# Two transformer blocks on one core: the last eight heads of block one divided by products with ones, and a denser start

## The chip, the cores and the metric

One NeuronCore of a Trainium2 chip runs the whole program; the other cores are idle. The metric is the device time of one execution in microseconds (us), and lower is better. All arithmetic is in float32. The engines are named as the profile names them: PE (TensorE; PEld is its weight load), DVE (VectorE), ACT (ScalarE), POOL (GpSimd), and SP, whose queue issues most of the transfers.

## The reference, cut to what matters

The input x is 2 x 1024 x 256, and a context of 2 x 64 x 256 goes with it. Two blocks follow each other, both with 16 heads of 16 channels:

```
# block 0
q = ln(x);                x = x + self_attention(q, q)             # 16 heads, softmax over 1024 keys
x = x + cross_attention(ln(x), ln(ctx))                            # 64 keys
h = ln(x); logits = h @ rw.T; top 2 of 8 experts, softmax gates
x = x + sum_k gate_k * (gelu(h @ fc1[e_k].T + b1) @ fc2[e_k].T + b2)
# block 1
x = x + self_attention(ln0(x));  x = x + cross_attention(ln1(x), ctx, mask)
x = x + gelu(ln2(x) @ fc1.T + b1) @ fc2.T + b2
```

A head's attention is exp(scores - largest) @ V, divided by the row's sum of exp. The division is what one part of the change computes in another way.

## The kernel before, in words

**Self-attention** (`self_attention`, used by both blocks as layer 0 and layer 1). Four heads are worked on at once: each has 32 rows of the 128, 16 of them channels. A "head group" h is four heads by 512 queries; there are 16 groups per block (batch, half of the queries, four groups of heads), and each has eight cells of 128 keys (or 128 queries by half the keys in the first pass), so 128 cells per block. A cell has three parts:

- pass "a" (L747): four products of queries and keys, whose only use is the largest score of each row; DVE reads each from a PSUM bank with a reduction (L754). It runs `LEAD` = 10 cells ahead of pass "b".
- pass "b" (L758): four products whose exp ACT writes to SBUF (L764). The largest score has been subtracted from the queries' tile (`largest`, L702 turns the maxima, L704 subtracts).
- `product` (L809): exp times V, where V has a column of ones at place 16 of its 20 columns, so that row 16 of each 32 is the sum of exp. ACT copies the sum (L818 the first, L821 the others), and POOL, or DVE once there are no more maxima to take, adds it to the group's accumulator `acc` (L822).

**The division before.** When a group is done, `finish` sends `acc` to DRAM (`send`, L470 and L471). After two groups it is gathered back with the heads side by side (L475); the sums are inverted on DVE (L486), go to DRAM (L487), come back spread over their heads' rows (`spread_out`, L491), and one multiplication divides (L497, on POOL while maxima are taken, else on DVE). `project` then multiplies by the output weights (L426) and adds to x (L434). The steps are put one cell apart by `at_cell`.

**What fills the gaps.** PE, DVE, ACT and SP are issued in the order in which the Python code records them (POOL's order is left to a scheduler). All other work is generators in a `Stream`: values, keys and queries of later groups (L594, L624), the norms (L358), the cross-attention (`weigh`: L1051, L1081, L1117, L1130, L1140, L1155), the dispatch of tokens to experts (`dispatch_task`) and the experts' slots (L1592 first layer, L1622 second). A generator yields its cost in us after a piece, or a wait (zero or less). In the loop over cells, `step` takes pieces by their due time as long as the budget `owed` lasts. Behind the loop `rest` empties the stream by rank and by the waits. `early` with `fill_up` does the same for the first ten cells of pass "a", which have no pass "b" beside them.

**Ends of the attention.** After cell 127 of block 0, only slot 0 of the experts can run at once: slots 1 to 4 need the counts of dispatch 2 (`found` 3), the rest need dispatch 3, which needs the last cross-attention, which needs the projection of the last two head groups (14 and 15).

The cross-attention already divides by products: `product(g)` at L1130 to L1149 multiplies by a 0/1 matrix `picks` to get the sums and inverts them, and `divided` (L1155, L1162) spreads the inverse by another 0/1 product.

Of the kernel before, what the change touches and what calls it, by code (L numbers as in the profile page):

```python
# [41 lines left out]
F32 = mybir.dt.float32  # L42
# [62 lines left out]


O_SUM, O_HEAD = 0, 128
NPICK = 640

W_O, W_V, W_Q, W_K = 0, 512, 1024, 1536  # L110
NSELF = 2048
# [17 lines left out]
class Stream:  # L129
# [46 lines left out]
    def rest(self, later, cell, mark=None):  # L176

        now, ready = 0.0, {}  # L180
        while (self.tasks or later) and (mark is None or mark not in self.made):
            for c in sorted(later):
                if (c - cell) * CELL <= now:
                    for go in later.pop(c):
                        go()
            tasks = [t for t in self.tasks if self.made.issuperset(t.after)]
            able = [t for t in tasks if ready.get(t, 0.0) <= now]
            if able:
                t = max(able, key=lambda t: (t.rank, -ready.get(t, 0.0)))
                cost = self.advance(t)  # L190
                if cost is not None:
                    now += max(0.0, cost)
                    ready[t] = now - min(0.0, cost)
            else:
                now = min([ready[t] for t in tasks] + [(c - cell) * CELL for c in later])
        return now
# [3 lines left out]
def two_blocks(  # L200
# [295 lines left out]
    def divide(dst, by):  # L496
        helper().tensor_tensor(dst, dst, by, ALU.mult)  # L497
# [17 lines left out]
    def self_attention(layer, tail, heads, arrive, extra, when_ready, beside=None):  # L515
# [30 lines left out]
        def at_cell(cell, go):  # L546
            later.setdefault(cell, []).append(go)
# [160 lines left out]
        def finish(h, cell):  # L708


            b, qh, g = h // 8, h // 4 % 2, h % 4
            if g == 0:
                ot[b, qh] = opool.tile([P, 2, 512], F32, tag="ot", name=f"ot_{names}{b}{qh}")
            if g % 2 == 0:
                sm = small.tile([P, 32], F32, tag="sums", name=f"sums_{names}{h}")
                sums[g // 2] = next_heads(), sm
            n, sm = sums[g // 2]
            dst = ot[b, qh][:, g // 2, :]
            send(acc.pop(h), n, g % 2, sm)
            if g % 2 == 1:  # L720
                by = opool.tile([P, 512], F32, tag="by", name=f"by_{names}{h}", bufs=1)
                gather(n, dst)
                at_cell(cell + 1, lambda: invert(n, sm))
                at_cell(cell + 2, lambda: spread_out(n, by))
                at_cell(cell + 3, lambda: divide(dst, by))
                if g == 3:
                    at_cell(cell + 4, lambda: project(b, qh))

        def project(b, qh):
            def go():  # L730
                for t0 in range(0, 4, 2):
                    yield from project_task(ot[b, qh], w, b * TB + 4 * qh + t0, t0, 2)
                when_ready(b, qh, stream, now[0])

            stream.add(go(), 4.0, last=now[0] + 4, rank=60)

        def score(kind, cell, j):
            h, n = divmod(cell, 8)
# [140 lines left out]
        add_values(1, 34, [("norm", 1)] + (["filled"] if layer == 0 else []))  # L879
        if layer == 0:  # L880

            fill_up(-LEAD, 2.0)
            owed = 0.0
            for ahead in range(0, LEAD, 2):
                cell = now[0] = ahead - LEAD
                for n, _ in enumerate(early(ahead)):
                    for go in later.pop(cell + n, []):
                        go()
                    if (ahead, n) == (6, 1):
                        collect(0)  # L890
                        stream.add(largest(0), 0.75, last=cell, mark=("QB", 0))
                        fill_up(cell, 1.0)
                        stream.until(("QB", 0))

                    owed += 0.7
                    while owed > 0.6 and (cost := stream.step(cell)):
                        owed -= cost
        owed = 0.0
# [143 lines left out]
    def weigh(layer, b, pool, w, name, held):  # L1042
# [124 lines left out]
        SC, LA, TU, PR, DI = scores, largest, weights_turned, product, divided  # L1167
        if maxima[0]:

            for now in (  # L1170
                ((SC, 0, 0), (LA, 0, 0)),
                ((LA, 0, 1),),
                ((SC, 0, 1), (LA, 0, 2)),
                ((TU, 0, 0), (LA, 0, 3)),
                ((SC, 1, 0), (LA, 1, 0)),
                ((TU, 0, 1), (LA, 1, 1)),
                ((PR, 0),),
                ((SC, 1, 1), (LA, 1, 2)),
                ((TU, 1, 0), (LA, 1, 3)),
                ((DI, 0),),  # L1180
                ((TU, 1, 1),),
                ((PR, 1),),
            ):
                for step, *args in now:
                    step(*args)
                us = {SC: cost, TU: 1.15, PR: 1.1, DI: 0.55}.get(now[0][0])
                if us:
                    yield us
                yield 0.0
            return  # L1190
        for step, *args, wait in (
            (SC, 0, 0, None),
# [751 lines left out]
def _layout(inputs):  # L1944
# [84 lines left out]
    for r in range(4):  # L2029
        for u in range(2):  # L2030
            for c in range(4):
                picks[SK * u : SK * (u + 1), O_SUM + 32 * r + 8 * c + 2 * r + u] = 1.0
    for c in range(4):
        for h in range(8):
            at = O_HEAD + c * P + DH * h
            picks[32 * c + h, at : at + DH] = 1.0
# [42 lines left out]
```

## Time and profile before

| what | value |
|---|---|
| time, median of 4 runs | 1637.29 us (1633.3 to 1640.46) |
| the profiled execution's own time | 1643.58 us |
| its span, first to last instruction | 1641.8 us |
| mean granted TensorE clock | 0.977 |
| PE busy | 1588.6 us (97%) |
| DVE busy / ACT busy / POOL busy | 981.8 / 911.3 / 414.7 us |
| first product of pass "b" in block 0 (L758) | 61.99 us |
| last product of block 0's attention (L809) begins | 596.58 us, for 3.24 us |
| first product of the last cross-attention of block 0 (L1051) | 638.18 us |

"Busy" of PE counts a matmul from its start to a modelled end, so it does not tell how fast PE went; the granted clock beside it does. A float32 matmul of the program stands in the trace as two records, so four matmuls are "x8". In the timelines each line has the start, the length, the engine, the line of the kernel, the operation with its tiles, the count, and in brackets the idle time before it and what ended that.

### The profile page before, as it was taken

Reading aid. Unit: us, or ns where it says so; the run is one execution under the profiler, and the core shown is the slowest. Engines: PE = TensorE matmul, PEld = TensorE weight load, DVE = VectorE, ACT = ScalarE, POOL = GpSimd, SP = SyncE. Lnnn points to the kernel's source line nnn. Section 1 sums busy time; section 2 is a strip of 40 time slices with the busy share of each in tenths; the row PEclk is TensorE's granted clock in tenths of the full one; section 3 lists DMA queues with packets and bytes.
Section 4 is the critical chain, followed back from the end, with each engine's and each line's share of the span. In section 5 each row is a group of like instructions: output and inputs, shape, how many; then the busy total and the mean of one; then the engine's idle time right before and its main releaser. Section 6 shows DMA issues by size and latency. Waiting matters only on the chain.

```text
span 1641.8 us, 28274 instructions
## 1 busy us (share of the span) xinstructions
PE 1588.6 (97%) x10682; PEld 875.4 (53%) x10682; DVE 981.8 (60%) x2092; ACT 911.3 (56%) x1768; POOL 414.7 (25%) x549
## 2 busy tenths in 40 slices
PE   7999999999999988999999989999999999999998
PEld 3333344444443446778888753344444435546766
DVE  5687857688687737431114456876767777845400
ACT  2277867667665763423322327876776676674321
POOL 2134324234334302141112032411322323321010
PEclk8799999999998999999999999999999999999999
DMA  4333510110000115176556321000110002000000
GB/s 142 123 131 114 180 35 21 27 34 31 30 21 27 60 56 194 68 259 224 180 200 237 97 65 34 21 28 14 40 40 21 21 14 82 15 14 21 14 13 26
DMA packets 56591, 122.09 MB, mean 74 GB/s; under 512 B 12546, under 2 KB 26756, under 8 KB 56068
## 3 DMA queue, kind: packets, MB, share of 16 engines
q1 hardware_dynamic: 52612, 110.08, 20.6%
q0 software_dynamic: 3456, 9.51, 1.6%
q8 instruction: 86, 1.41, 0.4%
q10 hardware_dynamic: 384, 0.66, 0.2%
q14 instruction: 53, 0.43, 0.1%
HBM read 72.14 MB, written 39.42 MB: 68 GB/s over the span
## 4 chain that ended last, share of the span: by engine, by line
PE 91%; DVE 6%; issue 1%; DMA 1%; ACT 1%; another core or an unknown queue 0%; POOL 0%; SPq 0%; DVEq 0%; POOLq 0%; ACTq 0%
PE banks L758 17%; PE banks L747 15%; PE banks L809 14%; PE banks L1592 8%; PE banks L1622 8%; PE banks L624 4%; PE banks L1764 3%; PE banks L1752 3%; PE banks L426 3%; PE banks L594 2%; PE banks L1051 2%; DVE mx_s L754 2%; PE banks L1081 2%; PE banks L1117 2%; PE banks L358 1%
## 5 line engine op out<-in xcount | busy, mean ns | idle before, releaser
L754 DVE TENSOR_REDUCE mx_s<-banks 128x1 f32<-128x512 f32 x1024 | 634.5, 682 | 211.1 <-PE banks L747 206.2
L764 ACT ACTIVATE pt_s<-banks 128x512 f32<-128x512 f32 x1024 | 531.0, 608 | 151.2 <-PE banks L747 125.9
L747 PE MATMUL banks<-KS,QS 16*128 16x512 f32 x2048 | 535.7, 632 | 3.8 <-issue 1.9
L758 PE MATMUL banks<-qb_s,KS 32*128 32x512 f32 x2048 | 509.9, 620 | 8.9 <-DVE qb_s L704 4.9
L822 POOL TENSOR_TENSOR acc_s<-acc_s,part_s 128x512 f32<-128x512 f32 x143 | 181.7, 1270 | 432.8 <-ACT part_s L821 420.9
L758 PEld LDWEIGHTS banks<-qb_s,KS 32*128 32x128 f32 x2048 | 177.1, 185 | 182.5 <-DVE mx_s L754 104.7
L809 PE MATMUL banks<-pt_s,v_s 128*20 128x512 f32 x2048 | 262.2, 604 | 0.7 <-DVE sc_c L1102 0.5
L747 PEld LDWEIGHTS banks<-KS,QS 16*128 16x128 f32 x2048 | 197.5, 186 | 78.5 <-issue 36.4
L1622 PE MATMUL banks<-w_slot,h_s 128*128 128x256 f32 x640 | 145.0, 383 | 2.9 <-ACT h_s L1598 2.9
L809 PEld LDWEIGHTS banks<-pt_s,v_s 128*20 128x20 f32 x2048 | 42.6, 98 | 181.8 <-ACT pt_s L764 129.6
L1622 PEld LDWEIGHTS banks<-w_slot,h_s 128*128 128x128 f32 x640 | 121.8, 192 | 23.5 <-ACT h_s L1598 3.3
L821 ACT COPY part_s<-banks 128x512 f32<-128x512 f32 x157 | 93.8, 598 | 61.7 <-PE banks L809 49.9
L1631 DVE SCALAR_TENSOR_TENSOR ys<-banks,gate,b 128x256 f32<-128x256 f32 x40 | 19.3, 484 | 169.9 <-PE banks L1622 166.9
L1598 ACT ACTIVATE h_s<-banks,w_slot 128x256 f32<-128x256 f32 x104 | 43.6, 470 | 119.0 <-issue 65.3
L1637 POOL DMA_INDIRECT results<-ys,to x40 | 38.7, 967 | 258.4 <-DVE ys L1631 176.3
L1592 PE MATMUL banks<-xsT,w_slot 128*128 128x256 f32 x416 | 95.7, 381 | 0.7 <-ACT xsT L365 0.7
L1592 PEld LDWEIGHTS banks<-xsT,w_slot 128*128 128x128 f32 x416 | 77.3, 190 | 14.8 <-DVE mx_s L754 2.3
L624 PE MATMUL banks<-xT_s,w_att 128*128 128x512 f32 x128 | 69.1, 676 | 0.0
L1755 ACT ACTIVATE h_f<-banks,w_ff 128x512 f32<-128x512 f32 x32 | 22.0, 687 | 73.9 <-PE banks L1752 73.9
L1102 POOL TENSOR_TENSOR sc_c<-sc_c,mx_c 128x512 f32<-128x512 f32 x38 | 39.5, 1042 | 77.6 <-DVE mx_c L1101 77.6
L1764 PE MATMUL banks<-w_ff,h_f 128*128 128x256 f32 x256 | 58.7, 387 | 0.0
L1598 ACT ACTIVATE h_s<-banks,spare 128x256 f32<-128x256 f32 x56 | 23.4, 471 | 63.2 <-issue 31.3
(260 smaller groups left out, 1646.8 us busy)
## 6 DMA issues: line engine op xcount, KB each, us to landing
w_slot<-in_ff_w_dram SPq DMA_DIRECT2D x40, 576.0 KB
sorted_rows<-fill SPq DMA_DIRECT2D x36, 520.0 KB
w_slot<-in_ff_w_dram SPq DMA_DIRECT2D x26, 514.0 KB
whole<-acc_s SPq DMA_DIRECT2D x32, 256.0 KB
spare<-in_ff_w_dram SPq DMA_DIRECT2D x14, 514.0 KB
xs<-sorted_rows SPq DMA_DIRECT2D x20, 260.0 KB
ot_s<-whole SPq DMA_DIRECT2D x16, 256.0 KB
by_s<-turns SPq DMA_DIRECT2D x16, 256.0 KB
```

Source lines behind the costliest of these rows:

```text
L624: nc.tensor.matmul(p, lhsT=w[:, at + k * D + pair * P : at + k * D + (pair + 1) * P], rhs=xT[b][:, k, blk * 512 : (blk + 1) * 512], start= ...
L747: nc.tensor.matmul(sc, lhsT=QS[h % 4][r, qc * P : (qc + 1) * P], rhs=K[r, kh * 512 : (kh + 1) * 512], start=True, stop=True,)
L754: return i, lambda: nc.vector.tensor_reduce(mx[h][:, qc, j, kh : kh + 1], sc, AX.X, ALU.max)
L758: nc.tensor.matmul(sc, lhsT=K[r, n * P : (n + 1) * P], rhs=QB[h][r, :], start=True, stop=True)
L764: nc.scalar.activation(pt, sc, AF.Exp, scale=SCALE)
L809: nc.tensor.matmul(o[32 * j : 32 * j + VW, :], lhsT=V[b][:, cell % 8, 4 * g + j, :], rhs=exps.pop((cell, j)), start=(cell == cells[0]), st ...
L821: nc.scalar.copy(part, o)
L822: helper().tensor_tensor(acc[h], acc[h], part, ALU.add)
L1592: nc.tensor.matmul(ph[:, n, :], lhsT=w[:, at : at + P], rhs=xT[:, k, :], start=(k == 0), stop=(k == 1),)
L1598: nc.scalar.activation(h1[:, f, :], ph[:, n, :], AF.Gelu, bias=w[:, W_B1 + f : W_B1 + f + 1])
L1622: nc.tensor.matmul(py, lhsT=h1[:, f, h * P : (h + 1) * P], rhs=w[:, f * D : (f + 1) * D], start=(f == 0), stop=(f == 7),)
L1764: nc.tensor.matmul(py[:, n, :], lhsT=h1[:, f, t * P : (t + 1) * P], rhs=w2[:, f * D : (f + 1) * D], start=(f == 0), stop=(f == 7),)
```

## The change

Five things, with all else the same:

1. Head groups 14 and 15 of block 0 (the last eight heads) no longer go through DRAM. `side_by_side` moves the rows of both accumulators together with a 0/1 matrix (two matmuls of 64 x 512), makes the sums with another (eight of 32 x 128), inverts them on DVE while ACT copies the heads, spreads the inverse (four of 128 x 128) and multiplies on DVE. Its rank in `rest` is 80, and the projection waits for it by a mark.
2. At the start of block 0 `fill_up` takes 4.0 us of the stream's work in place of 2.0, each early cell earns 1.4 us in place of 0.7, and 3.0 us more are taken between the last maxima and their turning.
3. In `weigh`, while maxima are taken, the second half's scores come before the first product, two steps are joined with others, and the waits after the end of the maxima are their own.
4. `rest` starts with the waits that the tasks already have, where it took all as ready.
5. While maxima are taken, the division on POOL and the projection are put one cell later.

`picks` grows from 640 to 768 columns.

```diff
-        now, ready = 0.0, {}
+        now, ready = 0.0, {t: (t.first - cell) * CELL for t in self.tasks}
...
+            if layer == 0 and h >= 8 * B - 2:
+
+                if g == 3:
+                    stream.add(
+                        side_by_side([acc.pop(h - 1), acc.pop(h)], ot[b, qh][:, 1, :]), 2.0,
+                        mark="compact", rank=80,
+                    )
+                    project(b, qh, ["compact"])
+                return
...
-                at_cell(cell + 3, lambda: divide(dst, by))
+
+                late = 3 + maxima[0]
+                at_cell(cell + late, lambda: divide(dst, by))
                 if g == 3:
-                    at_cell(cell + 4, lambda: project(b, qh))
-
-        def project(b, qh):
+                    at_cell(cell + late + 1, lambda: project(b, qh))
+
+        def side_by_side(parts, dst):
+
+            i, o = bank()
+            j, s = bank()
+            for half, part in enumerate(parts):
+                nc.tensor.matmul(
+                    o[64 * half : 64 * (half + 1), :], lhsT=picks[:, O_ROWS : O_ROWS + 64],
+                    rhs=part, start=True, stop=True,
+                )
+            for half, part in enumerate(parts):
+                for c in range(4):
+                    nc.tensor.matmul(
+                        s[32 * c : 32 * (c + 1), :P],
+                        lhsT=picks[:, O_PART + 32 * half : O_PART + 32 * (half + 1)],
+                        rhs=part[:, c * P : (c + 1) * P],
+                        start=(half == 0),
+                        stop=(half == 1),
+                    )
+            inv = small.tile([P, P], F32, tag="inv", name=f"inv_{names}", bufs=1)
+            nc.vector.reciprocal(inv, s[:, :P])
+            nc.scalar.copy(dst, o)
+            free.extend((j, i))
+            yield 1.5
+            yield -1.6
+            i, by = bank()
+            for c in range(4):
+                nc.tensor.matmul(
+                    by[:, c * P : (c + 1) * P],
+                    lhsT=picks[:, O_HEAD + c * P : O_HEAD + (c + 1) * P],
+                    rhs=inv, start=True, stop=True,
+                )
+            nc.vector.tensor_tensor(dst, dst, by, ALU.mult)
+            free.append(i)
+            yield 0.55
+            yield -1.0
+
+        def project(b, qh, after=()):
...
-            stream.add(go(), 4.0, last=now[0] + 4, rank=60)
+            stream.add(go(), 4.0, last=now[0] + 4, rank=60, after=after)
...
-            fill_up(-LEAD, 2.0)
+            fill_up(-LEAD, 4.0)
...
                         collect(0)
+                        fill_up(cell, 3.0)
                         stream.add(largest(0), 0.75, last=cell, mark=("QB", 0))
+                        stream.until(("QB", 0))
                         fill_up(cell, 1.0)
-                        stream.until(("QB", 0))
-
-                    owed += 0.7
+
+                    owed += 1.4
...
-                ((PR, 0),),
-                ((SC, 1, 1), (LA, 1, 2)),
-                ((TU, 1, 0), (LA, 1, 3)),
-                ((DI, 0),),
-                ((TU, 1, 1),),
-                ((PR, 1),),
+                (((SC, 1, 1), (LA, 1, 2)), 0.0),
+                (((PR, 0), (LA, 1, 3)), -1.5),
+                (((TU, 1, 0),), None),
+                (((DI, 0), (TU, 1, 1)), -1.4),
+                (((PR, 1),), None),
             ):
                 for step, *args in now:
                     step(*args)
-                us = {SC: cost, TU: 1.15, PR: 1.1, DI: 0.55}.get(now[0][0])
+                us = sum({SC: cost, TU: 1.15, PR: 1.1, DI: 0.55}.get(step[0], 0.0) for step in now)
                 if us:
                     yield us
-                yield 0.0
+                if maxima[0]:
+                    yield 0.0
+                elif wait is not None:
+                    yield wait
...
+    for j in range(4):
+        for d in range(DH):
+            picks[32 * j + d, O_ROWS + DH * j + d] = 1.0
+        for half in range(2):
+            for c in range(4):
+                picks[32 * j + DH, O_PART + 32 * half + 8 * c + 4 * half + j] = 1.0
```

## The prediction

> **What bounds the kernel now.** I read the page's head and chain first, then PE's busy time and clock by stretch, and then the timelines of the two stretches where PE is not full.
>
> ```profile
> PE 1588.6 (97%) x10682; PEld 875.4 (53%) x10682; DVE 981.8 (60%) x2092; ACT 911.3 (56%) x1768; POOL 414.7 (25%) x549
> PE 91%; DVE 6%; issue 1%; DMA 1%; ACT 1%; another core or an unknown queue 0%; POOL 0%; SPq 0%; DVEq 0%; POOLq 0%; ACTq 0%
> ```
>
> PE is the bound nearly everywhere, and the change leaves its work as it is but for some 2.5 us. So a gain can only come from PE's idle time and from the time at a low clock. Both sit in few places (columns: stretch, length, PE's busy us and records, granted clock, DMA share, GB/s):
>
> ```profile
> 30.00:40.00 10.00, 10.00 (x33) 0.67 0.01 2
> 40.00:50.00 10.00, 10.00 (x32) 0.67 0.00 0
> 50.00:60.00 10.00, 7.22 (x24) 0.50 0.33 52
> 60.00:70.00 10.00, 10.00 (x52) 0.94 0.42 142
> ```
> ```profile
> 480.00:520.00 40.00, 37.84 (x232) 0.90 0.04 14
> 520.00:560.00 40.00, 39.22 (x289) 0.98 0.16 51
> 560.00:600.00 40.00, 40.00 (x343) 1.00 0.11 39
> 600.00:640.00 40.00, 28.33 (x116) 0.85 0.35 115
> ```
>
> The start runs at half to two thirds of the clock though PE looks full; behind the first attention PE is idle for 11.7 us of 40. PE's timeline at the start:
>
> ```profile
> 24.14 2.60 PE L747 MATMUL banks<-KS,QS 16*128 16x512 f32 x8 [1.91 <-issue]
> 26.67 3.52 PE L594 MATMUL banks<-w_att,xT_s 128*128 128x256 f32 x8
> 35.93 3.78 PE L624 MATMUL banks<-xT_s,w_att 128*128 128x512 f32 x4
> 54.21 1.12 PE L702 MATMUL banks<-ident,spread 128*128 128x128 f32 x4 [2.78 <-DVE spread L782]
> 65.78 1.99 PE L594 MATMUL banks<-w_att,xT_s 128*128 128x256 f32 x8
> ```
>
> The same four L594 matmuls take 3.52 us at 26.67 and 1.99 at 65.78: the early ones run at half speed. DVE in that stretch needs 7.27 us for twelve reductions and then idles:
>
> ```profile
> 41.27 7.27 DVE L754 TENSOR_REDUCE mx_s<-banks 128x1 f32<-128x512 f32 x12 [2.62 <-PE banks L747]
> ```
>
> And PE behind the attention, with SP's issues of the round trip through DRAM:
>
> ```profile
> 605.76 1.97 PE L358 MATMUL banks<-ident,xd_m 128*128 128x128 f32 x8 [5.35 <-DVE xd_m L1255]
> 618.53 1.89 PE L426 MATMUL banks<-w_att,ot_s 128*128 128x256 f32 x8
> 632.34 0.76 PE L358 MATMUL banks<-ident,xn_c 128*128 128x128 f32 x4 [2.62 <-DVE over L1425]
> 635.63 0.69 PE L358 MATMUL banks<-ident,xn_c 128*128 128x128 f32 x2 [2.53 <-DVE xn_c L346]
> 638.18 2.08 PE L1051 MATMUL banks<-xT_c,w_att 128*128 128x512 f32 x2 [0.66 <-issue]
> ```
> ```profile
> 601.20 0.62 SPq L470 DMA_DIRECT2D sums_s<-acc_s  x1
> 608.04 0.33 SPq L487 DMA_DIRECT2D turns<-sums_s  x1
> 610.02 0.63 SPq L491 DMA_DIRECT2D by_s<-turns  x1
> ```
>
> Accumulators are whole at 601.17, the division (L497 on DVE) begins at 615.19, the projection at 618.53: 17 us on a round trip, of which slot 0's first layer hides most; its second layer is then gone when the norm of the last cross-attention needs cover.
>
> **Part 2, the start.** In the new recorded order four steps of L594 and not two stand ahead of the first L758, and both bias products too. The two L594 that move cost 1.92 us each in the chain at 65.85 and 77.58, the biases (L452, L456 from 69.63 to 72.7) 3.1: 6.9 us leave the loop, where PE is full. What the start then takes, from 24.14: ten groups of L747 at 1.05, three of L624 at 1.92 (99.72 in the chain), two L594 at 1.95, the biases 3.1, L702 0.7: 24 us at full clock. DVE needs 40 reductions at 0.61 (24.2 us), two copies of 0.42, the context's statistics 1.1, L782 and L704 0.9: 27 us. So DVE is the bound; one more L594 pair fills the 1.91 us before 24.14, another the 2.78 us at 51.4. The loop begins at about 24.1 + 28 = 52 and not at 61.99: 10 us earlier, with 6.9 us less to do, 16.9 in all. That is one end. The other is a clock that stays at half: 24 us of work cost some 45, the loop begins at 69, 7 us late, and the 6.9 us moved make it nothing. I take 14, near the first end: the dense L624 at 57.27 is followed by full clock from 61 on, and the new order never has more than two groups of L747 without a full-width matmul between them. ACT's and SP's extra steps (two copies of 0.58, no transfer) lie in their idle time.
>
> The Trainium skill ("TensorE: Matmul & The Clock Gate", Part 1, the HAM clock gate) says that a window of about 3.4 us of busy PE releases the full clock; by it the sum would be the 16.9 us. Its section "A second HAM failure mode: psum-queue depth-cycling" speaks against the change: where PE waits in short steps for PSUM banks, as a start paced by DVE does, the clock swings back, and the sum would be nearer to zero. The rows at 30 to 50 us, full by their look and at 0.67, side with the second for stretches of L747 alone.
>
> **Part 3, the cross-attention's order, and part 5.** PE's and DVE's pieces are the same and stand one or two cells elsewhere. Where dispatch or statistics meet a cell without PE pieces (2.94 us of PE; four reductions alone are 2.42 of DVE), DVE falls behind. Before, that costs PE 1.39 us at 504.58 and 0.76 at 509.25, and a stretch at clock 0.90. Adding the rows' durations cell by cell, DVE exceeds PE by 14.7 us over block 0's loop before and by 18.7 in the new order (new at cells 67 to 69, 77 to 79, less at 108): 4 us more, of which banks ahead absorb some. Bounds: 0 and, with the clock at half behind each gap, 25; I take +2, as before 14.7 us of excess made under 6 us of gaps. The new order is also two cells shorter: the projection of cross-attention 2 ends at cell 124, not 126, so dispatch 2 begins while the attention still runs. POOL's division keeps its place between the same two additions, so its wait of 7.19 us for the spread inverse at 147.74, and the 1.19 us that PE loses behind it, stay. The projection one cell later delays nobody in the order. In block 1 the excess is 7.1 and 7.2 us: nothing.
>
> **Part 1 and 4, the tail.** Let T = 599.8, the end of the last L809. ACT's copy and DVE's addition end at T+1.4 as before; PE waits for them. Two 64 x 512 and eight 32 x 128 products: by the like L1130 and L1140 (0.9 and half of 0.87) 1.3 us if the halves run side by side, 2.3 if not: T+3.2. The transposes of dispatch 2 (0.9; its statistics are done by then) fill part of the reciprocal (0.75 to 0.96 by L1149). The spread by L1155 0.9, T+5.3; DVE's multiplication 0.7, T+6.2; two projections of 1.82, with L1268 between, to T+11.7. Slot 0's first layer (three quarters, 5.2 us) covers DVE's hots; DVE, now without a break, does the four statistics and the roots of the last norm by T+22 and its first pair by T+24.3, about 1.6 us after PE's pieces end. L1051 starts at T+30.3 in place of T+38.4, with slot 0 wholly done in both: 8 us, though 2.5 us of PE work are new. The transfers removed are eight on SP; slot 0's second weights move ahead on that queue, and nobody waits for them. `picks` is 64 KB larger, needed far later.
>
> What is late next: the last cross-attention. Before, 4.6 us of slot 1 (eight and eight L1592, 1.73 each, and L1558 1.1) fill it; the new order has none before its last scores, and DVE paces it (eight times 0.69 and 0.69). Ends: 4.6 us lost, or 2.6 won, as ACT no longer changes tables for gelu there (1.28 us each at 651.39 and 656.09). I take 2 lost, nearer to DVE's pace. The tail gains 6; its ends are 0 and 11 (with the clock of 0.85 restored).
>
> **The sum.** -14 + 2 - 6 = -18 against the profiled execution's own 1643.58: 1625.6. That execution lies 6.3 above the median of the runs, so 1637.29 - 18 = 1619.3 there.
>
> **The rivals.**
> - The start stays at half clock: 0 + 2 - 6, 1633. For it: 0.67 at 30 to 50. Against: the full clock after dense L624.
> - The tail's gain is eaten by the unfilled cross-attention: -14 + 2, 1625. For it: the DVE waits there; against: the table changes saved.
> - All goes well: -16.9 - 11 + 0, 1609.
> - Slower: DVE becomes the pace of block 0's loop. Each gap of 1 to 2 us is followed by up to 10 us at half clock (0.90 over 480 to 520 and 0.98 over the next 40 make that together), some 4.3 us lost each. Place: cells 67 to 69, 77 to 79, 105 to 107, 109 to 115. Five gaps cost 4 + 5 x 4.3 = 25 against gains of 14 + 6: 1637.3 - 20 + 25 = 1642; four about balance them. For it: 18.7 against 14.7. Against: one such stretch before, with 14.7.
> - The change does not do what it says: the order rules it out, as L470 to L491 are gone for groups 14 and 15.
>
> **Chances.** Forecast 0.53, 1609 0.10, tail 0.13, half clock 0.13, slower 0.11. A difference under 0.3% (4.9 us) can't be told from none, so the half-clock case is half "same". Faster 0.82, same 0.07, slower 0.11. The range leaves out the outer half of the best case and most of the slower one: 1607 to 1635. The forecast's own is 1612 to 1627.
>
> **What would show it.** First L758 at 51 to 55 us, clock over 0.8 from 30 to 60; L1051 of the last cross-attention some 30 us behind the last L809; no gap of 5 us there; the gaps at 500 to 510 about as before. Wrong if the clock at 30 to 60 us is still 0.6, if new gaps by L754 stand in the loop with stretches at half clock, or if the last cross-attention lasts over 20 us.

## The result, and the profile after

The changed kernel takes 1636.49 us in the median of 44 executions (1627.19 to 1641.8), the kernel before 1636.34 in the median of 70 (1626.6 to 1653.08). The ratio is 0.9985, with a 95% interval of 0.9973 to 0.9997: some 2.5 us faster by the ratio, while the two medians differ by 0.15 us the other way. Either is below the 0.3% that can be told from no change, and the median lies above the upper end of the predicted range (1635). A later comparison (after_again below) gave 0.9982 (0.9959 to 1.0006).

The profiled execution of the changed kernel took 1633.51 us (span 1631.7, mean granted clock 0.981), that of before 1643.58. Ten microseconds between two traces, and 2.5 between many executions: a single trace of this kernel is not its median. What differs from one execution to the next is told under "unexpected" below.

The page's busy times of the changed kernel:

```profile
PE 1586.5 (97%) x10710; PEld 881.8 (54%) x10710; DVE 982.0 (60%) x2094; ACT 912.2 (56%) x1767; POOL 409.7 (25%) x545
```

PE has 28 records more, two for each of the 14 new products, and DVE two more. PE at the start and around the end of block 0's attention, stretch by stretch (stretch, length, PE's busy us and records, granted clock, DMA share, GB/s):

```profile
30.00:40.00 10.00, 10.00 (x54) 1.00 0.38 64
40.00:50.00 10.00, 8.90 (x52) 1.00 0.79 303
50.00:60.00 10.00, 10.00 (x37) 0.60 0.35 139
60.00:70.00 10.00, 10.00 (x54) 0.72 0.01 2
```
```profile
480.00:520.00 40.00, 37.37 (x244) 1.00 0.08 27
520.00:560.00 40.00, 39.10 (x282) 0.88 0.19 62
560.00:600.00 40.00, 37.84 (x310) 0.96 0.09 30
600.00:640.00 40.00, 34.52 (x175) 0.86 0.41 134
```

The start now runs at full clock until 50 us. Half clock comes after that, when the loop begins. Behind the attention PE is busy for 34.5 of 40 us where it was 28.3, but the clock there is no better (0.86, it was 0.85). The row up to 600 us holds 9 us that lie behind the attention; ahead of its end PE is busy for 30.74 of 30.91 us. PE's timeline at the start, and DVE's:

```profile
27.12 1.14 PE L796 MATMUL banks<-KS,QS 16*128 16x512 f32 x8
28.19 1.98 PE L626 MATMUL banks<-xT_s,w_att 128*128 128x512 f32 x4
43.82 1.99 PE L596 MATMUL banks<-w_att,xT_s 128*128 128x256 f32 x8
46.91 0.66 PE L704 MATMUL banks<-ident,spread 128*128 128x128 f32 x4 [1.10 <-DVE spread L831]
49.70 1.72 PE L807 MATMUL banks<-qb_s,KS 32*128 32x512 f32 x4
```
```profile
34.25 9.66 DVE L803 TENSOR_REDUCE mx_s<-banks 128x1 f32<-128x512 f32 x16 [0.50 <-PE banks L796]
48.96 6.06 DVE L803 TENSOR_REDUCE mx_s<-banks 128x1 f32<-128x512 f32 x10
```

The first product of pass "b" (L807 in this kernel, L758 before) begins at 49.70 and not at 61.99. A group of L596 takes 1.99 us where an early one took 3.52 before, and DVE does its reductions back to back. Behind the attention:

```profile
593.90 1.17 PE L747 MATMUL banks<-acc_s,picks 128*64 128x512 f32 x2 [1.99 <-DVE acc_s L871]
599.29 2.14 PE L428 MATMUL banks<-w_att,ot_s 128*128 128x256 f32 x8
622.36 3.60 PE L1101 MATMUL banks<-xT_c,w_att 128*128 128x512 f32 x8
629.71 3.10 PE L1131 MATMUL banks<-kbd,q_c 32*128 32x128 f32 x32 [3.75 <-ACT q_c L1108]
650.75 3.72 PE L1644 MATMUL banks<-xsT,w_slot 128*128 128x256 f32 x16
```

T is again the end of the attention's last product (L858, L809 before): 590.91 here, 599.82 before. The projection begins at T+8.4 (before: T+18.7), the last cross-attention's first matmul (L1101, before L1051) at T+31.45 (before: T+38.36). But then PE waits 3.75 us for ACT, and the first expert work that could fill the cross-attention (slot 1, L1644) stands behind most of it, at T+59.8. Block 1's first product of pass "b" follows 368.64 us behind T; before, it followed 368.80 behind it. All that the tail had won is lost again. The last cross-attention takes 34.6 us from its first matmul to its projection (L428 at 656.92); before, it took 28.9 (L426 at 667.03).

### The profile page after: what moved, and what is told of

The parts are those of the page before. It is cut to its first block, busy times and chain, and to the rows that moved or that the text cites. A ratio compares the mean times of both kernels' runs of the same rounds, so it can differ in the third digit from the quotient of the medians.

```text
span 1631.7 us, 28319 instructions
## 1 busy us (share of the span) xinstructions
PE 1586.5 (97%) x10710; PEld 881.8 (54%) x10710; DVE 982.0 (60%) x2094; ACT 912.2 (56%) x1767; POOL 409.7 (25%) x545
## 5 line engine op out<-in xcount | busy, mean ns | idle before, releaser
L807 PE MATMUL banks<-qb_s,KS 32*128 32x512 f32 x2048 | 517.5, 622 | 6.6 <-DVE qb_s L706 3.7
L807 PEld LDWEIGHTS banks<-qb_s,KS 32*128 32x128 f32 x2048 | 180.8, 186 | 178.7 <-DVE mx_s L803 104.9
L858 PE MATMUL banks<-pt_s,v_s 128*20 128x512 f32 x2048 | 263.8, 607 | 1.5 <-DVE mx_s L803 1.0
L858 PEld LDWEIGHTS banks<-pt_s,v_s 128*20 128x20 f32 x2048 | 43.3, 99 | 186.6 <-ACT pt_s L813 131.6
L1644 PE MATMUL banks<-xsT,w_slot 128*128 128x256 f32 x416 | 95.6, 381 | 0.7 <-ACT xsT L367 0.7
L1644 PEld LDWEIGHTS banks<-xsT,w_slot 128*128 128x128 f32 x416 | 77.4, 190 | 14.9 <-DVE mx_s L803 2.3
L626 PE MATMUL banks<-xT_s,w_att 128*128 128x512 f32 x128 | 61.6, 616 | 0.0
```

Of the source, the lines that this page charges most:

```text
L626: nc.tensor.matmul(p, lhsT=w[:, at + k * D + pair * P : at + k * D + (pair + 1) * P], rhs=xT[b][:, k, blk * 512 : (blk + 1) * 512], start= ...
L807: nc.tensor.matmul(sc, lhsT=K[r, n * P : (n + 1) * P], rhs=QB[h][r, :], start=True, stop=True)
L858: nc.tensor.matmul(o[32 * j : 32 * j + VW, :], lhsT=V[b][:, cell % 8, 4 * g + j, :], rhs=exps.pop((cell, j)), start=(cell == cells[0]), st ...
L1644: nc.tensor.matmul(ph[:, n, :], lhsT=w[:, at : at + P], rhs=xT[:, k, :], start=(k == 0), stop=(k == 1),)
```

## The experiments

"Part 1" to "part 5" are those of the list above. "Lost to the clock" is the span times (1 - mean granted clock) of an execution. Half-clock stretches stand in the traces with a clock of 0.50 and are 3.4 us long or a multiple of it (one at the end of the span is cut off), so each costs PE at most half its length. Ratios are to executions of the kernel before on the same chip, with 95% intervals; each kernel has 6 to 12 executions. A ratio can move by more than its interval says when the chip changes: the one kernel with part 2 alone gave 0.9893 and 0.9957, and these two intervals do not overlap.

| kernel | parts | median, us | before beside it | ratio | lost to the clock, median |
|---|---|---|---|---|---|
| before_again | none | 1636.98 | 1638.01 | 0.9984 (0.9961 to 1.0007) | 35.1 |
| start_alone | 2 | 1620.96 | 1638.01 | 0.9893 (0.9864 to 0.9923) | 25.9 |
| start_again | 2 | 1627.29 | 1637.09 | 0.9957 (0.9924 to 0.9989) | 30.1 |
| tail_alone | 1, 4 | 1637.17 | 1638.01 | 1.0004 (0.9980 to 1.0028) | 34.4 |
| loop_alone | 3 | 1643.61 | 1638.01 | 1.0036 (1.0016 to 1.0057) | 34.5 |
| late_alone | 5 | 1632.75 | 1630.42 | 1.0014 (1.0000 to 1.0029) | 27.7 |
| start_and_tail | 1, 2, 4 | 1625.67 | 1637.09 | 0.9928 (0.9905 to 0.9951) | 27.6 |
| start_and_late | 2, 5 | 1620.89 | 1630.42 | 0.9933 (0.9910 to 0.9956) | 22.7 |
| start_and_loop | 2, 3 | 1633.23 | 1640.03 | 0.9966 (0.9937 to 0.9995) | 31.8 |
| start_and_loop_2 | 2, 3 | 1628.79 | 1630.42 | 0.9982 (0.9964 to 0.9999) | 28.5 |
| all_but_loop | 1, 2, 4, 5 | 1630.94 | 1640.03 | 0.9938 (0.9912 to 0.9964) | 27.7 |
| all_but_late | 1 to 4 | 1621.92 | 1637.09 | 0.9907 (0.9878 to 0.9936) | 20.3 |
| all_but_late_2 | 1 to 4 | 1616.35 | 1630.42 | 0.9925 (0.9897 to 0.9953) | 19.4 |
| after_again | all | 1636.28 | 1637.09 | 0.9982 (0.9959 to 1.0006) | 35.1 |
| start_swapped | 2, the exchange of 3 | 1630.61 | 1640.03 | 0.9940 (0.9913 to 0.9967) | 31.0 |
| start_joined | 2, one join of 3 | 1627.34 | 1640.03 | 0.9934 (0.9908 to 0.9960) | 27.6 |
| late_but_11 | all, but not group 11 of 5 | 1626.34 | 1640.13 | 0.9922 (0.9894 to 0.9950) | 27.6 |
| late_only_11 | 1 to 4, group 11 of 5 | 1632.29 | 1640.13 | 0.9950 (0.9930 to 0.9970) | 27.7 |

### Each part by itself, and before once more

> The kernel before, unchanged, to learn how far its executions differ and what in them differs. Theory A (the profiled execution of before was an unlucky one): span times mean granted clock stays at 1604 us within 1 in all executions, while the time lost to the half clock, 37.7 us in the profiled one, is nearer to 31 in the median execution; the half-clock stretches at 27 to 61 us, 27.3 us long there, are shorter in the new trace. Theory B (the start is always at half clock): the new trace shows 20 us or more at half clock before 61 us again, and the median loses 37.

Theory A (an unlucky trace) falls. The new trace is even slower (span 1645.6, clock 0.972), the start is at half clock again, 27.3 us of it before 62 us, and the median loses 35.1 us to the clock, nearer to theory B's 37 than to 31. Span times clock is 1600.4 in the median (1595.1 to 1601.6). So what the change wins at the start was no luck. What varies is the time behind it: the two traces differ by 0.1 us at cell 80, and by 5.0 at cell 96, all of it one half-clock stretch of 10.2 us at 416 us that the first trace did not have. Note the ratio of the same kernel to itself: 0.9984. The 0.9985 of the whole change is no more than that.

The denser start:

```diff
-            fill_up(-LEAD, 2.0)
+            fill_up(-LEAD, 4.0)
...
                         collect(0)
+                        fill_up(cell, 3.0)
...
-                    owed += 0.7
+                    owed += 1.4
```

> Part 2 alone (the denser start). By the prediction's own term: 14 us faster, 1622 to 1624. By theory A, that most of the term was an unlucky clock in one execution: span times clock falls by 4 to 5 us (the idle PE that the start saves), the clock's loss stays near that of before, 1631 to 1633. By theory C, that the start's gain is real but given back in the loop whatever the order there: pass b begins at 50 us as in the changed kernel, and the lead over before falls by 5 us or more between cells 60 and 124 here too; 1630.

> Part 2 alone once more, on another chip and beside the kernel with all parts. If its 17 us are the start's own: 1.0% faster than before again, 1621 to 1624. If they were luck of one chip (where the low clock falls): 0.6 to 0.8% faster, as the two kernels that differ from it by one detail of the order.

1.07% faster on one chip (17.5 us), 0.43% on another (7 us, 1.8 to 12.4). The first is more than any theory said, the second has the size that theory A named (1631 to 1633 beside 1638), though not its reason, and lies below both cases of its own expectation (0.6 to 0.8%, and 1.0%); theory C's loss in the loop is not there, as start_alone keeps its lead over before_again from cell 32 to cell 96 within 0.3 us (14.5 and 14.3). The traces say what of this is steady: in five traces with the old start, cell 48 begins at 248.7 to 251.7 us, in the fifteen with the new one at 233.8 to 241.2; the means are 250.6 and 237.0, so 13.6 us are won there. The two traces of the one kernel with part 2 alone agree at cell 48 (236.4 and 236.2) and end 11.4 us apart (1627.1 and 1615.8): lost to the clock were 32.4 and 18.8. Their PE windows at 400 to 600 us, first start_alone:

```profile
400.00:600.00 200.00, 192.24 (x1411) 0.92 0.11 36
```
then start_again:
```profile
400.00:600.00 200.00, 191.37 (x1453) 0.98 0.12 37
```

PE's busy share is the same; the clock is 0.92 and 0.98. Of the 6.3 us between the two medians, 4.2 are lost to the clock (25.9 and 30.1).

Parts 1 and 4 alone (the side-by-side step, and the starting waits, with the division and projection elsewhere at their old place):

```diff
-        now, ready = 0.0, {}
+        now, ready = 0.0, {t: (t.first - cell) * CELL for t in self.tasks}
...
+            if layer == 0 and h >= 8 * B - 2:
...
+                        side_by_side([acc.pop(h - 1), acc.pop(h)], ot[b, qh][:, 1, :]), 2.0,
```

> Parts 1 and 4 alone (side by side, and the starting waits). By the prediction's term: 6 us faster, 1630. By what the two traces show (lead 8.5 at the end of the attention, 15.8 at the last cross-attention's first matmul, 9.0 some 70 us later): the gain is given back behind the cross-attention, 0 to 1 us faster, 1636, with the wait of ACT and the half clock there again.

No gain, as the second expectation said: 1.0004. In its trace L1100 (the last cross-attention's first matmul) comes at T+33.9 in place of T+38.4 to 38.9, and block 1's first product of pass "b" at T+368.0 in place of 368.8 to 369.7. The wait of ACT that this expectation named is not there. There is a half-clock stretch of 10.2 us at 635.

The cross-attention's order alone, with two pairs of steps joined in one cell and the second half's scores ahead of the first product (cut to the lines that move; the numbers are waits that count once there are no more maxima to take):

```diff
-                ((PR, 0),),
-                ((SC, 1, 1), (LA, 1, 2)),
-                ((TU, 1, 0), (LA, 1, 3)),
-                ((DI, 0),),
-                ((TU, 1, 1),),
...
+                (((SC, 1, 1), (LA, 1, 2)), 0.0),
+                (((PR, 0), (LA, 1, 3)), -1.5),
+                (((TU, 1, 0),), None),
+                (((DI, 0), (TU, 1, 1)), -1.4),
```

> Part 3 alone (the cross-attention's order while maxima are taken). By the prediction's term: 2 us slower, 1638. By theory D, that the lead which the changed kernel loses between cells 60 and 124 (8 us, 3.4 of it clock and 2.5 of it work moved) is this order's doing: 4 to 8 us slower, 1640 to 1644. If the loss there is work that merely stands elsewhere: the same, 1636.

0.36% slower, 5.9 us (2.6 to 9.3): theory D's size. The PE windows in which it happens, first of before_again, then of loop_alone (columns as above):

```profile
360.00:400.00 40.00, 39.82 (x275) 1.00 0.07 20
520.00:560.00 40.00, 40.00 (x282) 0.93 0.12 42
```
```profile
360.00:400.00 40.00, 38.77 (x224) 0.91 0.06 16
520.00:560.00 40.00, 38.06 (x257) 0.91 0.12 41
```

New idle time of PE, 1.1 and 1.9 us, and in the first window also a new half-clock stretch (6.8 us at 386). Between cell 48 and T, PE idles 1.8 to 4.0 us in the six traces with the old order and the old place of the division, in one to four gaps of over 0.25 us; in the five with the new order and the old place of the division it idles 5.1 to 5.3 us, in six gaps, and DVE ends nearly all of it (5.0 to 5.1 us). Idle time is thus 1 to 3 us of the 5.9. The medians do not show the rest as half clock: 34.5 us are lost to it, as before (34.4 on that chip), while span times clock is 1609.0 and not 1601.4. Where the rest lies, no run shows.

### Where the rest goes

Taken together, the single parts make about the whole: some -12 (the mean of the two runs of part 2), +5.9, +0.7 and, from late_alone below, +2.3, which is -3; measured is -2.5. But they do not add up in company, as the next runs show.

The changed kernel with the cross-attention's old order, and parts 2 and 3 without the others:

> The changed kernel with the cross-attention's order of before (parts 1, 2, 4 and 5). Alone, the start gave 17 us, the loop's order cost 5.6 and the tail nothing, which add up to 1627; the changed kernel takes 1636.5, so some 10 us are lost between the parts. Theory D (part 3 together with the new start costs them): 1621 here. Rival E (the tail or part 5 together with the new start costs them): 1630 or more here.

> Parts 2 and 3 alone. Theory D: 1635 to 1637, with 34 us lost to the half clock in the median as in the changed kernel (the start alone lost 26). Rival E: the sum of the two parts, 1626 to 1628, and 26 us lost to the clock.

Neither theory holds as put. The kernel before takes 1640.03 on this chip and not 1636.34, so the ratios tell more than the numbers: 0.9938 lies between theory D's 1621 (0.991) and rival E's 1630 (0.996), and 0.9966 between E's 1626 to 1628 (0.994 to 0.995) and D's 1635 to 1637 (0.999 to 1.000). Some of the loss needs part 3, and some needs the tail or part 5.

Two details of part 3, each with part 2: first the exchange (start_swapped), then one join (start_joined).

```diff
-                ((PR, 0),),
                 ((SC, 1, 1), (LA, 1, 2)),
+                ((PR, 0),),
```
```diff
-                ((DI, 0),),
-                ((TU, 1, 1),),
+                ((DI, 0), (TU, 1, 1)),
```

> Part 2 and of part 3 only the exchange: the second half's scores stand before the first product, no steps are joined, so that a cross-attention is as long as before. If the joined steps are what DVE or PE can't take in one cell: 1621, as the start alone. If the exchange is (two steps of scores with one between them, where a product stood): 3 us or more slower than the start alone, 1624 and up.

> Part 2 and of part 3 only one join: the first division stands in one cell with the last turning, a cross-attention is one cell shorter. If the joined steps cost (1.7 us of PE and 0.7 of DVE more in one cell, and all that follows one cell earlier, among it the dispatch): 3 us or more slower than the start alone, 1624 and up. If not: 1621.

0.9940 and 0.9934: by time the two can't be told apart, nor from the start alone on two chips. The traces do tell them apart: between cell 48 and T PE idles 2.5 us in two gaps with the exchange, and 5.5 us in seven gaps with the join, 5.46 of it ended by DVE. So the gaps of part 3 come with the shorter cross-attention; that they are also what costs the time is not shown by these two medians.

Now without part 5, and with the start and the tail alone:

```diff
-                late = 3 + maxima[0]
+                late = 3
```

> The changed kernel once more, beside the start alone. By its earlier runs 0.15% faster than before; the start alone is then 0.5 to 0.9% faster than this kernel, which is what the other parts cost together.

> Parts 1, 2 and 4, without the cross-attention's order and without the later division. With the later division the same took 0.62% less than before, the start alone 1.07% less. If part 5 costs the difference: 1621, as the start alone. If the tail does: 1630.

> The changed kernel with the division and the projection at their old place (parts 1 to 4). If part 5 costs: 4 us or more faster than the changed kernel, 1632 or less. If the cross-attention's order alone costs: 1635 to 1637.

The changed kernel without part 5 is 0.93% faster than before, on the same chip on which the changed kernel is 0.18% faster. Part 5, which moves a division and a projection by one cell and adds no work, takes some 12 us there. (The start alone was to be 0.5 to 0.9% faster than the changed kernel; on this chip it is 0.25%.) The start and the tail without part 5 lie between the two cases expected, and are no faster than with it (0.9928, and all_but_loop on another chip 0.9938). So part 5 seems to cost only with part 3. To see whether that holds, and what part 5 does by itself:

> Parts 1 to 4 once more. If part 5 is what takes the gain: 0.6 to 1.2% faster than before, as the first time (0.93%), and some 20 us lost to the half clock in the median where the changed kernel loses 34. If the first time was luck: 0.2 to 0.5% faster.

> Part 5 alone. Theory F (it is no work, and costs only where other gaps then fall in a bad place): within 0.3% of before. Theory G (POOL's and PE's work one cell later costs by itself): 0.3 to 0.8% slower, 1641 to 1650.

> Parts 2 and 5. Theory F: 0.4 to 1.1% faster than before, as the start alone on two chips. Theory G: 0 to 0.4% faster.

> Parts 2 and 3 once more, beside parts 1 to 4. If the tail (1 and 4) gives nothing in company either, as alone: the same as parts 1 to 4 within 0.3%. If it gives its predicted 6 us there: 0.35% slower than those.

Parts 1 to 4 are again 0.75% faster, with 19 us lost to the clock where the changed kernel loses 34 to 35. Part 5 alone costs 0.14% (0 to 0.29), with the start nothing that shows: theory F, not G. And parts 1 and 4, which give nothing alone, give 0.57% (9 us) once part 3 is there: 0.9982 without them, 0.9925 with them, on one chip. The expectation had 0 or 6 us; it is the second, and more. On these chips the kernel before loses 34.2 to 34.4 us to the clock.

### The step of part 5 that does it

The tail of the kernel without part 5 (all_but_late_2), PE's timeline; its T is 584.88:

```profile
587.00 1.60 PE L360 MATMUL banks<-ident,xd_m 128*128 128x128 f32 x8 [2.11 <-DVE xd_m L1307]
588.52 1.98 PE L747 MATMUL banks<-acc_s,picks 128*64 128x512 f32 x4
615.23 3.60 PE L1101 MATMUL banks<-xT_c,w_att 128*128 128x512 f32 x8
618.75 1.72 PE L1131 MATMUL banks<-kbd,q_c 32*128 32x128 f32 x32
633.72 1.89 PE L1644 MATMUL banks<-xsT,w_slot 128*128 128x256 f32 x8
637.41 3.72 PE L1644 MATMUL banks<-xsT,w_slot 128*128 128x256 f32 x16
```

Here the transposes of dispatch 2 (xd_m) stand ahead of the side-by-side step (L747), at T+2.1; in the changed kernel they stand behind it, at T+5.1:

```profile
596.01 1.97 PE L360 MATMUL banks<-ident,xd_m 128*128 128x128 f32 x8
```

All that dispatch 2 leads to comes sooner with them. Slot 1's rows are fetched (xs on SP's queue) at T+35.4 in place of T+41.4, in the changed kernel and in this one:

```profile
632.26 2.16 SPq L1558 DMA_DIRECT2D xs<-sorted_rows  x3
```
```profile
620.31 2.28 SPq L1558 DMA_DIRECT2D xs<-sorted_rows  x3
```

So slot 1 fills the last cross-attention from T+48.8 on, where the changed kernel has it at T+59.8. PE's windows of 20 us at that place, the changed kernel and then all_but_late_2:

```profile
620.00:640.00 20.00, 15.46 (x89) 0.72 0.77 254
```
```profile
620.00:640.00 20.00, 17.35 (x190) 1.00 0.75 275
```

What in part 5 can reach dispatch 2? Head group 11 (the last of the third quarter of the queries): its projection gives the input of the last cross-attention but one, and that the input of dispatch 2. In all_but_late_2 that last projection but one begins 15.8 us ahead of T, in both traces of the changed kernel 12.9 us, and the dispatch then comes too late to stand ahead of the side-by-side step. The projection, in all_but_late_2 and then in the changed kernel:

```profile
569.05 3.72 PE L428 MATMUL banks<-w_att,q_c 128*128 128x256 f32 x16
```
```profile
578.04 3.72 PE L428 MATMUL banks<-w_att,q_c 128*128 128x256 f32 x16
```

With the old order of part 3 the transposes come late anyway, part 5 or not: at T+10.5 in tail_alone, T+8.9 in start_and_tail, T+10.1 in all_but_loop. That fits what the times say: without part 3 the tail has little to win, and part 5 nothing to undo. The two kernels that part this step from the rest of part 5, against the changed kernel: first late_but_11, then late_only_11.

```diff
-                late = 3 + maxima[0]
+                late = 3 + (maxima[0] and (layer, h) != (0, 11))
```
```diff
-                late = 3 + maxima[0]
+                late = 3 + ((layer, h) == (0, 11))
```

> All parts, but head group 11 of block 0 is divided and projected at its old place; the order at the end of the attention is then that of parts 1 to 4. Theory H (that one step holds back dispatch 2 and so the expert work that fills the last cross-attention): 0.6 to 1.0% faster than before, as parts 1 to 4; the dispatch's transposes begin some 2 us behind the last product, slot 1's rows are fetched 35 us behind it. Theory F (part 5 moves gaps about, no place in particular): 0.1 to 0.5%.

> Parts 1 to 4, and of part 5 head group 11 of block 0 alone. Theory H: the gain falls to that of the changed kernel, 0.1 to 0.3% faster than before; the dispatch's transposes begin 5 us behind the last product, slot 1's rows are fetched 41 us behind it, ACT's wait of 7 us ahead of the last cross-attention's queries is there again. Theory F: 0.5 to 0.9% faster.

late_but_11: 1626.34 us beside 1640.13, 0.9922 (0.9894 to 0.9950), as without part 5. late_only_11: 1632.29, 0.9950 (0.9930 to 0.9970). In the trace of late_but_11 (T = 589.51) the dispatch is back at T+2.1 and slot 1's rows at T+34.1:

```profile
591.61 1.41 PE L360 MATMUL banks<-ident,xd_m 128*128 128x128 f32 x8 [2.11 <-DVE xd_m L1307]
```
```profile
623.59 2.40 SPq L1558 DMA_DIRECT2D xs<-sorted_rows  x3
```

The trace of late_only_11 has all three signs of theory H: the dispatch at T+5.5 (T = 589.54), slot 1's rows at T+41.3, and ACT's wait:

```profile
595.06 1.70 PE L360 MATMUL banks<-ident,xd_m 128*128 128x128 f32 x8
628.33 3.10 PE L1131 MATMUL banks<-kbd,q_c 32*128 32x128 f32 x32 [3.73 <-ACT q_c L1108]
```
```profile
627.59 1.26 ACT L1108 ACTIVATE q_c<-banks,cols 128x512 f32<-128x512 f32 x2 [7.10 <-remote]
```

Its first product of pass "b" in block 1 comes at T+368.5, as in the changed kernel (T+368.6 in both traces); in late_but_11 it comes at T+360.9, in the two traces of parts 1 to 4 at T+361.4 and T+355.3. Theory H holds for the place: this one step costs 7 to 13 us of the tail in the traces. Half clock can be 6.8 to 8.5 us of that: from T to block 1's first product 20.5 us are at half clock in late_only_11, 3.4 to 6.8 in late_but_11 and the two traces of parts 1 to 4. For the size, theory H holds in one direction only. Taken out of the whole change, the step gives 0.60 to 0.63% (0.9922 against 0.9982 and 0.9985), nearly all that part 5 costs beside part 3 (0.57 to 0.78%). Put in alone, it takes 0.25 to 0.43% (4 to 7 us, against all_but_late and all_but_late_2), short of what theory H named. Each of these differences is uncertain by about 0.3% or more, so the step is 4 to 10 us, and whether it is all of part 5 stays open. It also costs in the loop: late_only_11 idles 9.1 us of PE between cell 48 and T, where the traces of parts 1 to 4 idle 5.3. For more of part 5 than this step there is a sign in the traces only: from cell 48 to T the three with part 3 and the whole or nearly whole part 5 need 355.7 to 356.7 us, late_only_11 353.2, five with part 3 and without part 5 349.5 to 352.9, six with neither 343.3 to 352.0.

Parts 1 to 4 without part 5 are thus better than both kernels: 0.75 and 0.93% faster than before in two comparisons, where the whole change gains 0.15 and 0.18%.

## Why the prediction went wrong, step by step

**The sum beside the two profiled executions.** Up to cell 48 the changed kernel is 16.5 us ahead of before (234.2 and 250.7). From cell 48 to T it loses 7.6 (356.7 and 349.1), from T to block 1's first product of pass "b" it wins 0.2, and behind that 1.0: together the 10.1 us between the two spans. So the -14 held, and the other two terms failed: +2 came as +7.6, and -6 as -0.2. That the medians lie closer still than these two executions do is the luck of single executions.

**The start: the size right, the path only up to 50 us.** 14 us were taken, 13.6 measured at cell 48. Pass "b" begins at 49.7 and 52.1 in the two traces of the changed kernel (52 was worked out, 51 to 55 named, so one is a little early), DVE is the pace as worked out (9.0 and 9.8 us busy in 30 to 50 us). The clock is over 0.8 up to 50 us only; at 50 to 60 it is 0.60. The stretch at half clock moved to where the loop begins: 13.7 or 17.1 us long, from 51.6 to 58.0 us on, in all fifteen traces with this start. There DVE still has ten reductions to do without a break (6.06 us at 48.96). The Trainium skill ("TensorE: Matmul & The Clock Gate", "A second HAM failure mode: psum-queue depth-cycling") tells of a kernel whose clock swings where PE idles briefly between its groups as it goes through the PSUM banks. By the sum that the prediction set beside it the gain would have been near zero. The trace agrees that the clock falls there, and not on the size: what the stretch costs, at most 6.8 to 8.5 us, is already in the 13.6. Whether the banks are the reason is not shown: PE counts as busy there for 10.00 of 10 us.

**The cross-attention's order: the mechanism right, the size too small.** The term was +2, between 0 and 25. Alone it measured +5.9. Idle time behind DVE grew by 1 to 3 us, as the sum of the rows had it (4 us more, some absorbed). The other 3 to 5 us are in no term of the prediction, and where they come from stays open; the median of loop_alone loses no more to half clock than before (34.5 and 34.4).

**Part 5: the failed step.** The prediction says "The projection one cell later delays nobody in the order", and costs part 5 at nothing. It delays dispatch 2. The first statistics of this dispatch do begin ahead of T (T-8.5), as the prediction says. But the projection of cross-attention 2 begins 12.9 us ahead of T and not 15.8, the last statistics end at T-1.3 where without part 5 they end at T-5.6, and the transposes come at T+5.1 and not T+2.1, behind the side-by-side step. The prediction read that order as it stands (the transposes "fill part of the reciprocal"); it did not ask what stood there without part 5. The chain of group 11 was followed to its projection and no further. The experiments put 4 to 10 us on this one group, and 9 to 13 on all of part 5 in the company of part 3.

**The tail: right up to the last cross-attention, mis-sized behind it.** L1101 was worked out for T+30.3, and came at T+31.45 and T+31.48. The term took 8 us off and 2 back for a cross-attention with nothing to fill it, between 4.6 lost and 2.6 won. From L1101 to block 1's first product it took 337.2 us, where before it took 330.4: the 2 measured 6.8, more than the lower end. Of these, 5.7 are in the cross-attention itself (34.6 us up to its projection, 28.9 before), which holds ACT's wait with 3.75 us of PE's, and 13.7 us at half clock. With dispatch 2 ahead of the side-by-side step it takes 28.4 to 30.9 us (all_but_late_2, all_but_late, late_but_11), the whole tail gains 7.4 to 13.5 us in the traces of parts 1 to 4, and parts 1 and 4 give 9 us by time: more than the 6 predicted. The sign named for this, a last cross-attention of over 20 us, could not tell: by this count the one before lasts 28.9.

**The rivals.** The one that let the unfilled cross-attention eat the tail came true, and the one that let DVE pace the loop came true in part. Each was given by itself, 1625 and 1642. The kernel did both at once, and no case in the prediction had that. The rival's price of a half-clock stretch, 4.3 us, is a little low: the two rows that it names make 4.8 (0.10 and 0.02 of 40 us), and that stretch is 10.2 us long, so it costs at most 5.1.

**The base.** The sum was made against one execution of 1643.58 and carried over to the median. For the start that was fair: the old one has lost 13.7 us or more to the clock by cell 16 in all five traces. Further on it isn't: between cell 48 and T the clock took 5.1 us in that trace, 12.0 in the next one of the same kernel, and 0 in a kernel with the same order.

## What to carry to other kernels

Where the order of the work is written down or planned, a step that moves by one place is followed to the end of the chain it feeds, not to its own consumer: here one projection, one cell later, undid much of what two other parts had won. Work that fills a gap has to be kept in it. A wait that ends sooner is worth only the idle time and the low clock that PE is spared until the next stretch in which PE is full, not its own lead: the last cross-attention began 6.9 us sooner, and block 1 0.2 us. And the parts of a change are priced together: here a part that cost next to nothing alone took 9 to 13 us beside another, and a part that gave nothing alone gave 9.

## What the runs showed of the hardware that was not expected

**The clock makes the spread.** Executions of one kernel on one chip differ by up to 24 us (start_again: 1616.28 to 1640.14), though the span times the granted clock is nearly the same in all of them: 1592 to 1597 there, while 19 to 44 us are lost to the clock. Whether a gap is followed by a half-clock stretch, and how long that is, changes from one execution to the next. Lengths are multiples of 3.4 us (3.4, 6.8, 10.2, 13.7, 17.1, and once 37.5), which agrees with the window in the Trainium skill ("TensorE: Matmul & The Clock Gate", Part 1). Between kernels the loss is no measure of time: late_alone loses 27.7 us where the kernel before loses 34.2 on the same chip, and is not faster, as its span times clock is 8 us more (1603.7 and 1595.7).

**ACT waits 7 us for something that the trace doesn't name.** In all three traces in which dispatch 2 stands behind the side-by-side step with the new order, ACT begins L1108 6.5 to 6.6 us after L1101 begins, where it takes 1.9 us in tail_alone (waits of 7.12, 6.98 and 7.10 us, "remote"). It starts 1.65 to 1.81 us after the start of POOL's additions of the bias (L420) each time. What it waits for stays open; no run was made for it.

**A copy of 16 columns takes 3.2 us on DVE.** In late_only_11, DVE's copy and POOL's additions:

```profile
625.16 3.20 DVE L1509 COPY end<-ntu 128x16 f32<-128x16 f32 x1
```
```profile
625.84 2.48 POOL L420 TENSOR_TENSOR x_sb<-x_sb,bias_out 128x512 f32<-128x512 f32 x2
```

The copy ends at 628.36, POOL's two additions at 628.32; in the trace of after_again the same copy takes 0.17 us and the addition behind it (L1510) 3.06, again up to the end of POOL's. The Trainium skill ("SBUF — State Buffer", "Who interferes with whom") says that a DVE copy in a mode that uses both ports, or an addition with both inputs in SBUF, can contend with a POOL instruction for a pair of ports that one of them holds for the whole instruction. The rows agree in that both end with POOL's additions. They do not show who took hold first: both DVE instructions begin ahead of the additions, by 0.68 and 0.53 us.
